# Two mixtures of experts: transposes moved a product ahead, a fixed VectorE order at the end, two tiles of returned rows added by a diagonal product, and next weights that wait for the rows

## The chip, the cores and the metric

The kernel runs on one core of one Trainium2 chip. The metric is device time in microseconds, the median of several runs. TensorE does the matrix products and the transposes, VectorE, ScalarE and GpSimd the rest, and SyncE issues the plain weight loads. In the profile these engines are PE (with PEld for its weight loads), DVE, ACT, POOL and SP.

## The reference, cut to what matters

A network of four layers works on x, 512 rows of 768 float32 values. Each layer adds a graph network and an attention-like mixer, both of the layer-normalised x, and then a feed-forward part, again of the layer-normalised x. The feed-forward parts of layers 0 and 2 are mixtures of experts; these two are what the change touches. With `xt` the normalised rows (512 x 768), 8 experts and a hidden width of 384:

```python
logits = xt @ Ws + bs
routes = argmax(softmax(logits), axis=-1)            # one expert for each row
prob_max = max(softmax(logits), axis=-1)
h = act(xt @ W1[routes] + b1[routes])                # gelu in layer 0, silu in layer 2
out = (h @ W2[routes] + b2[routes]) * prob_max
x = x + out
```

The next layer begins with a layer norm of this x.

## The kernel before, in words

x stays in SBUF as four tiles of 128 rows. A mixture (`moe`, L681) first writes the normalised x to DRAM (`there`), computes each row's expert, and sorts the rows by expert into blocks of 128 places, so that a block belongs to one expert. There are at least 4 and at most 11 blocks; blocks 0 to 8 are always computed (NA is 9), blocks 9 and 10 only under an `If` that reads their number from a register (L862, L869). Each engine reads that register and branches for itself.

Block i has two halves. `first(i)` (L826) gathers the block's rows `xb` and its expert's two weight matrices `w1` and `w2` by indirect DMAs on POOL's queue, transposes `xb` in six pieces into `xbT`, multiplies by `w1` (12 passes, since a float32 product takes two) and copies the result to `h`. `second(i)` (L844) transposes `h` in three pieces, applies the activation and bias on ScalarE (`hT`, L850), multiplies by `w2` (12 passes) and copies the result to `y`, half by VectorE and half by ScalarE (`copy`, L230). ScalarE's queue then stores `y` in DRAM (`back`, L859). The weights go into six buffers of the pool `wp`, shared with all other weight loads.

The loop at L864 calls `first(i + 1)`, then `second_bias` (a product with the 8-row bias table that is added to x, L815), then `second(i)`. So TensorE's order for one turn is: transposes of `xb(i+1)`, `w1(i+1)`, bias, transposes of `h(i)`, `w2(i)`. Instructions run in that order on the engine; a product that reads a copy has to wait for the engine that makes it.

After the loop come the `If`, four gathers of finished rows (`yb`, one for each tile of x, L875) from `back`, and `second(8)`. Block 8 isn't stored: its rows go straight to their places by a product with a placement matrix, `wayT` (L881), 16 passes in all. For every tile VectorE adds the two halves of that product to x (L360) and then the gathered rows times a factor `left`, which is zero for rows of block 8 (L883). What sets VectorE's order here is a scheduler with planned times, which mixes these additions with the statistics of the next norm.

The next norm (`norm1`, L344: two `bn_stats`, `bn_aggr`, a square root on ScalarE, a reciprocal, and on VectorE the scaled copy `xn`) belongs to the next stage. After layer 0's mixture that stage starts with `fold` (L1070 ff.): 72 passes of six weight tiles `g_t` with a small padded matrix `wq`, which POOL fills with a memset (L1075) and a copy (L1076). Its passes use tiles 1 to 3 in the first half and 4 to 6 in the second. Then `xn` is transposed. After layer 2's mixture the stage (`last_two`, L1398) begins with the norm, a small product of `wf` and `lr` (`fold3`, L1466), twelve small VectorE copies `V` out of it (L1482), and the transposes of `xn`. In both cases SyncE's queue issues six weight tiles ahead (L242), each as soon as one of the six `wp` buffers is free.

Of the kernel before, what the change touches and what calls it, by code (L numbers as in the profile page):

```python
# [10 lines left out]
F32 = mybir.dt.float32  # L11
BF16 = mybir.dt.bfloat16
I16 = mybir.dt.int16
I32 = mybir.dt.int32
AF = mybir.ActivationFunctionType
OP = mybir.AluOpType
# [4 lines left out]
P = 128  # L21
N = 512
NT = N // P
# [141 lines left out]
class Net:  # L165
    def __init__(self, ctx, tc, dram, at, out):
# [41 lines left out]
        self.onesb = keep.tile([P, P], BF16, name="onesb")  # L208
        nc.gpsimd.memset(self.onesb, 1.0)
        self.lower = keep.tile([P, P], BF16, name="lower")  # L210
        with tc.tile_pool(name="init", bufs=1) as ip:
# [26 lines left out]
    def w(self, ap, pool=None):  # L238

        parts, n = ap.shape  # L240
        t = (pool or self.wp).tile([P, WB], F32, tag="w", name="w")
        self.nc.sync.dma_start(t[:parts, :n], ap)  # L242
        return t
# [119 lines left out]
    def counts(self, c0, g0):  # L363
# [10 lines left out]
        with ExitStack() as c:  # L374
# [13 lines left out]
            worth = one.tile([P, 3, EJ], F32, name="worth")  # L388
            add = one.tile([P, EJ], F32, name="add")
            for n, ((e, u), (f, v)) in enumerate((((3, 0), (3, 1)), ((3, 2), (3, 3)), ((2, 0), (2, 1)))):  # L390
# [58 lines left out]
            for h in range(2):  # L449
                digit = {}  # L450
                for g in range(2):
# [29 lines left out]
                    for q in range((2 * h + g) * EJ // 8, (2 * h + g + 1) * EJ // 8):  # L481
                        features(q)
        over = self.small.tile([P, NT], BF16, name="over")
        nc.vector.tensor_scalar(over, most, 256.0, None, OP.is_gt)
# [144 lines left out]
    def attention0(self, nodesT):  # L629
        nc, tc, d = self.nc, self.tc, self.d  # L630
        ns = self.chunks(nodesT)
        with ExitStack() as c:
            att = c.enter_context(tc.tile_pool(name="g0_att", bufs=1))
            two = c.enter_context(tc.tile_pool(name="g0_two", bufs=2))
            masks = self.masks(c.enter_context(tc.tile_pool(name="mk", bufs=2)))
            v = att.tile([P, NT, D], F32, name="v")
# [43 lines left out]

    def moe(self, f, act, bs=None):  # L681

# [4 lines left out]
        with ExitStack() as c:  # L687
            one = c.enter_context(tc.tile_pool(name=f + "_one", bufs=1))
            two = c.enter_context(tc.tile_pool(name=f + "_two", bufs=2))
            xn = one.tile([P, NT, D], F32, name="xn")  # L690
            xnT = one.tile([P, KC, N], F32, name="xnT")
# [119 lines left out]
            nc.vector.tensor_copy(wayT, p)  # L811
            nc.vector.tensor_mul(left, left, pr)
            b2 = self.row(d[f + "_b2"], parts=8)

# [10 lines left out]

            def first(i):  # L826
                xb = two.tile([P, D], F32, name="xb", bufs=3)
                nc.gpsimd.indirect_dma_start(out=xb, out_offset=None, in_=there,
                                             in_offset=bass.IndirectOffsetOnAxis(ap=who[:, i : i + 1], axis=0))
                w1 = pick(d[f + "_w1"], i).rearrange("p (k n) -> p k n", k=KC)  # L830
                w2 = pick(d[f + "_w2"], i).rearrange("p (k n) -> p k n", k=3)
                xbT = two.tile([P, KC, P], F32, name="xbT")
                for k in range(0, KC, 3):
                    p = self.ps()
                    for j in range(3):
                        self.tr(p[:, j * P : (j + 1) * P], xb[:, (k + j) * P : (k + j + 1) * P])
                    self.copy(xbT[:, k : k + 3, :], p[:, :HW].rearrange("p (k n) -> p k n", k=3))
                p = self.ps()
                self.acc(p[:, :HW], [(xbT[:, k, :], w1[:, k, :]) for k in range(KC)])
                h = two.tile([P, HW], F32, name="h" if i < NA else "hm")  # L840
                self.copy(h, p[:, :HW])
                return h, w2

            def second(i, h, w2):  # L844
                hT = two.tile([P, 3, P], F32, name="hT")
                p = self.ps()
                for k in range(3):
                    self.tr(p[:, k * P : (k + 1) * P], h[:, k * P : (k + 1) * P])
                for k in range(3):
                    nc.scalar.activation(hT[:, k, :], p[:, k * P : (k + 1) * P], act, bias=bias[:, i, k, :])  # L850
                y = two.tile([P, D], F32, name="y")
                for nb in range(2):
# [8 lines left out]

            count = nc.values_load(more[:1], min_val=4, max_val=NB)  # L862
            held = first(0)
            for i in range(NA - 1):  # L864
                after = first(i + 1)
                second_bias(i // 2, i % 2)
                second(i, *held)
                held = after
            with tc.If(count > NA):  # L869
                for i in range(NA, NB):  # L870
                    second(i, *first(i))
            ys = []
            for t in range(NT):
                ys.append(two.tile([P, D], F32, name="yb", bufs=NT))
                nc.gpsimd.indirect_dma_start(out=ys[t], out_offset=None, in_=back,  # L875
                                             in_offset=bass.IndirectOffsetOnAxis(ap=slot[:, t : t + 1], axis=0))
            y = second(NA - 1, *held)
            for t in range(NT):
                for nb in range(2):
                    p = self.ps()  # L880
                    self.acc(p[:, :HW], [(wayT[:, t * P : (t + 1) * P], y[:, nb * HW : (nb + 1) * HW])])  # L881
                    self.add_x(t, nb, p[:, :HW])
                nc.vector.scalar_tensor_tensor(self.x[:, t, :], ys[t], left[:, t, :], self.x[:, t, :], OP.mult, OP.add)  # L883

# [184 lines left out]

    def fold(self, pool, l, H):  # L1070


        nc, d = self.nc, self.d
        wq = pool.tile([P, KC, 32], F32, name="wq")
        nc.gpsimd.memset(wq, 0.0)  # L1075
        nc.gpsimd.tensor_copy(wq[:, :, : 2 * H], self.col(f"g1_qk{l}", 0, KC * 2 * H).rearrange("p (k h) -> p k h", k=KC))  # L1076

# [119 lines left out]
    def gnn1(self, V1, xnT):  # L1197
        nc, tc, d = self.nc, self.tc, self.d
        with ExitStack() as c:
# [30 lines left out]

            products, turn2 = self.fold(one, 2, 1)
            with tc.tile_pool(name="g1_ex", bufs=2) as self.elu:
# [165 lines left out]
    def last_two(self, xn, xnT, out):  # L1398
# [5 lines left out]
        with ExitStack() as c:  # L1404
            one = c.enter_context(tc.tile_pool(name="m3_one", bufs=1))
            two = c.enter_context(tc.tile_pool(name="m3_two", bufs=2))
            self.norm(self.x, xn)
            V = self.fold3(one)
# [388 lines left out]
def tile_net(ctx, tc, dram, at, out, only=ALL):  # L1797
# [10 lines left out]
    with ExitStack() as ck, ExitStack() as c0:  # L1808
# [15 lines left out]
        if "gnn0" in only:  # L1824
            net.attention0(nodesT)
    if "ffn0" in only:
        net.moe("f0", AF.Gelu, "f0_bs")
    with tc.tile_pool(name="L1", bufs=1) as pool, ExitStack() as keep:
        xnT = pool.tile([P, KC, N], F32, name="xnT")
        right = keep.enter_context(tc.tile_pool(name="L1n", bufs=1, side="right"))  # L1830
        xn = right.tile([P, NT, D], F32, name="xn")
        aT = right.tile([P, KC, N], F32, name="aT")
        V1 = pool.tile([P, KC, 3, 8], F32, name="V1")
        products, turn = net.fold(right, 1, 4)
        net.norm(net.x, xn)
        vt = products(right)
# [9 lines left out]
    with tc.tile_pool(name="L2", bufs=1) as pool:  # L1846
# [3 lines left out]
        if "gnn2" in only:  # L1850
            net.gnn2(xn, xnT)
    if "ffn2" in only:
        net.moe("f2", AF.Silu)
    with tc.tile_pool(name="f3_x", bufs=1) as last:

        xn = last.tile([P, NT, D], F32, name="xn")
        xnT = last.tile([P, KC, N], F32, name="xnT")
        net.ffn3(xn, xnT, net.last_two(xn, xnT, xn))
# [23 lines left out]
```

## Time and profile before

| | |
|---|---|
| median of 3 runs | 4313.59 us (4308.73 to 4316.22) |
| the profiled execution | 4315.56 us, span 4313.8 us, mean granted TensorE clock 0.986 |
| layer 0's mixture, first `xb` transposes to the end of `w2(7)` | 1253.8 to 1351.05 us of the span |
| its end: `fold` starts, `fold` ends | 1373.80, 1383.53 us |
| layer 2's mixture, the same | 2845.0 to 2939.76 us |
| its end: last `xn` done, first product of the next stage with `xnT` | 2967.06, 2969.66 us |
| last stage: first weight load issued | 3168.83 us |

In a timeline, a line is a group of like instructions of one engine: start and length in microseconds, engine, line of the kernel, operation, output and inputs, number of instructions, and in brackets the engine's idle time before it and what ended it. The ends of matmuls are modelled: a row's end lies a little after the moment when the next product could start. The granted clock is 1.00 at full speed and 0.50[...].

### The profile page before, as it was taken

What the parts mean: (1) busy time and instruction counts of PE and PEld (TensorE: products, weight loads), DVE (VectorE), ACT (ScalarE), POOL (GpSimd) and SP (SyncE); (2) the same over time, 40 slices, a digit from 0 to 9 for tenths busy, and PEclk for the clock granted to TensorE, in tenths of its full rate; (3) what the DMA queues carried; (4) which work ended last, traced back from release to release, by engine and by line L of the source; (5) the groups of instructions that cost most, each with busy time, mean ns of one, the idle gap of its engine ahead of it and who ended that gap; (6) DMA issues with size and microseconds to landing.
All of it is one profiled execution on the core that took longest, in us unless ns stands there. A gap on an engine that the chain in (4) does not pass through costs nothing. (4 is left out here: it accounts for less than half of the span.)

```text
span 4313.8 us, 40131 instructions
## 1 busy us (share of the span) xinstructions
PE 4125.5 (96%) x16376; PEld 2099.9 (49%) x16376; DVE 1305.0 (30%) x3120; ACT 650.1 (15%) x1233; POOL 270.3 (6%) x316
## 2 busy tenths in 40 slices
PE   7989999999988999999999999978989999999998
PEld 3434555554444666755644444444554444444443
DVE  7772111112332125623220101035752122122211
ACT  2121200001211223421200000012610000000000
POOL 1120000001022010000000000021100000000000
PEclk9999999999989999999999999989999999999999
DMA  3111011111047112211211111063069999999998
GB/s 110 52 62 56 22 44 66 66 55 53 20 178 269 44 63 71 99 52 46 105 43 66 44 56 55 0 255 129 12 257 419 419 420 420 420 417 420 419 421 362
DMA packets 98956, 710.30 MB, mean 165 GB/s; under 512 B 12032, under 2 KB 12097, under 8 KB 29393
## 3 DMA queue, kind: packets, MB, share of 16 engines
q1 hardware_dynamic: 77776, 601.13, 35.1%
q0 software_dynamic: 16512, 93.97, 5.8%
q10 hardware_dynamic: 4480, 12.58, 0.8%
q8 instruction: 132, 2.16, 0.2%
q14 instruction: 56, 0.45, 0.0%
HBM read 685.09 MB, written 22.54 MB: 164 GB/s over the span
## 5 line engine op out<-in xcount | busy, mean ns | idle before, releaser
L1724 PE MATMUL ps<-w,xg 128*64 128x384 f32 x3072 | 566.0, 489 | 4.2 <-DMA w<-in_f_Wg_dram 2.1
L1724 PEld LDWEIGHTS ps<-w,xg 128*64 128x64 f32 x3072 | 234.1, 137 | 296.2 <-issue 271.1
L1356 PE MATMUL ps<-aT,w 128*128 128x512 f32 x864 | 372.3, 592 | 0.0
L1740 PE MATMUL ps<-w,hT 128*64 128x384 f32 x1536 | 320.7, 490 | 7.4 <-DMA w<-in_f_Wd_dram 3.1
L312 PE MATMUL ps<-xnT,w 128*128 128x512 f32 (+1 forms) x732 | 322.6, 598 | 0.2 <-ACT xnT L236 0.2
L1356 PEld LDWEIGHTS ps<-aT,w 128*128 128x128 f32 x864 | 164.2, 190 | 203.6 <-issue 202.3
L360 DVE TENSOR_TENSOR x<-x,ps 128x384 f32<-128x384 f32 x240 | 131.6, 552 | 329.6 <-PE ps L312 259.6
L312 PE MATMUL ps<-w,xnT 128*128 128x384 f32 x672 | 221.7, 486 | 0.2 <-DVE xnT L234 0.2
L312 PEld LDWEIGHTS ps<-xnT,w 128*128 128x128 f32 (+1 forms) x732 | 134.5, 185 | 175.9 <-issue 172.4
L1740 PEld LDWEIGHTS ps<-w,hT 128*64 128x64 f32 x1536 | 131.9, 136 | 170.8 <-issue 145.0
L312 PE MATMUL ps<-w,hT 128*128 128x384 f32 x552 | 189.4, 499 | 8.8 <-ACT hT L850 8.8
L312 PE MATMUL ps<-C,parts 128*128 128x512 bf16 x864 | 188.8, 380 | 2.5 <-DVE inv L1378 2.5
L463 PE MATMUL ps<-ohd,so 128*128 128x512 bf16 x816 | 182.1, 383 | 2.8 <-DVE so L460 2.8
L312 PEld LDWEIGHTS ps<-w,xnT 128*128 128x128 f32 x672 | 127.0, 190 | 88.6 <-issue 4.8
L1366 DVE TENSOR_TENSOR aT<-inv,ps 128x512 f32<-128x512 f32 x72 | 49.4, 686 | 365.7 <-PE ps L312 365.7
L1727 ACT ACTIVATE h<-ps 128x384 f32<-128x384 f32 x64 | 31.4, 490 | 794.0 <-PE ps L1724 794.0
L1728 DVE TENSOR_TENSOR h<-h,ps 128x384 f32<-128x384 f32 x64 | 35.4, 553 | 376.5 <-PE ps L1724 369.3
L312 PEld LDWEIGHTS ps<-w,hT 128*128 128x128 f32 x552 | 105.4, 194 | 83.9 <-ACT hT L850 13.7
L312 PE MATMUL ps<-w,aT 128*128 128x384 f32 (+1 forms) x416 | 139.6, 486 | 0.5 <-DVE aT L234 0.4
L312 PEld LDWEIGHTS <-parts 128*128 128x128 bf16 x864 | 84.8, 98 | 108.1 <-issue 8.8
L312 PE MATMUL ps<-xnT,sw 128*128 128x512 f32 x288 | 136.7, 605 | 0.0
L460 DVE TENSOR_SCALAR so<-io,ind,worth 128x256 bf16<-128x256 int16 x408 | 121.7, 356 | 35.6 <-PE ps L463 35.5
(487 smaller groups left out, 4787.7 us busy)
## 6 DMA issues: line engine op xcount, KB each, us to landing
w<-in_f_Wg_dram SPq DMA_DIRECT2D x128, 1152.0 KB, 14.5
w<-in_f_Wu_dram SPq DMA_DIRECT2D x128, 1152.0 KB, 14.4
w<-in_f_Wd_dram SPq DMA_DIRECT2D x128, 1152.0 KB, 15.2
w<-in_g_w_dram SPq DMA_DIRECT2D x54, 1152.0 KB, 5.1
w<-in_m_wqkv_dram SPq DMA_DIRECT2D x24, 1152.0 KB, 6.7
w<-in_g_t_dram SPq DMA_DIRECT2D x12, 1152.0 KB, 5.6
w<-in_m_wp_dram SPq DMA_DIRECT2D x8, 1152.0 KB, 5.3
ea<-in_edge_attr_dram SPq DMA_DIRECT2D x34, 256.0 KB, 2.7
```

What stands on the lines that cost most here:

```text
L312: self.nc.tensor.matmul(out, a, b, start=n == 0, stop=n == len(pairs) - 1)
L360: self.nc.vector.tensor_add(xs, xs, p)
L460: nc.vector.tensor_scalar(so[:, n, :], io[:, h * 256 : (h + 1) * 256], ind[:, 0, j : j + 1], worth[:, n, j : j + 1], OP.is_equal, OP.mult)
L463: nc.tensor.matmul(p, so[:, n, t * P : (t + 1) * P], ohd[:, j, :], start=False, stop=j == (g + 1) * HJ - 1)
L1356: nc.tensor.matmul(outs[nb * 3 + f], w[:, k, f * P : (f + 1) * P], xT[:, k, :], start=first and k == 0, stop=last and k == KC - 1)
L1366: nc.vector.tensor_mul(aT[:, f, :], inv[:, r, :], p)
L1724: nc.tensor.matmul(p[a * 64 : a * 64 + 64, :HW], xg[:, k, a * CAP : (a + 1) * CAP], ws[b][a][:, k, :], start=k == 0, stop=k == KC - 1)
L1727: nc.scalar.activation(h, pg[:, :HW], AF.Silu)
L1728: nc.vector.tensor_mul(h, h, pu[:, :HW])
L1740: nc.tensor.matmul(po[nb][a * 64 : a * 64 + 64, :HW], hT[:, f * P + a * 64 : f * P + a * 64 + 64], wd[a][:, f, nb * HW : (nb + 1) * HW], s ...
```

## The change

- The expert loop. `first` is split into `fetch` (gathers and the transposes of `xb`) and the product with `w1`; `second` is split into `middle` (the transposes of `h` and the activation) and the product with `w2`. One turn is now: `middle(i)`, `w1(i+1)`, `fetch(i+2)`, bias, `w2(i)`. `middle(8)` stands ahead of the `If`. The blocks under the `If` have their own `hTm` buffer.
- The end. The eight halves of the placement product go into eight PSUM tiles, all issued one after another. For tiles 2 and 3 of x, the gathered rows are added in the same PSUM tiles by a product with a diagonal matrix that holds `left` (`diag`); tiles 0 and 1 keep VectorE's multiply-add. VectorE's order is written out: each of its instructions is told to be issued after the one before it (`turn`). The next norm is part of this sequence, and its scaled copy moves to ScalarE as an Identity activation with scale r and bias -mean r.
- Next weights. The fifth of the plain weight loads that follow the mixture gets a dependence on the last gather of returned rows; the sixth and later ones stand behind it on SyncE's queue.
- The padded matrix of layer 1's `fold`, now `wq1`, is filled near the start of the program and kept.
- `xn` is a tile of the caller, on the other side of SBUF in layer 0. A small tile `add` in the first stage shares the rotating buffers called `so`, and `over` moves to a lasting pool.

```diff
 def w(self, ap, pool=None):
-    self.nc.sync.dma_start(t[:parts, :n], ap)
+    i = self.nc.sync.dma_start(t[:parts, :n], ap)
+    if self.gate is not None:
+        if self.before == 0:
+            self.tc.add_manual_dep(i.ins, self.gate.name, mybir.DependencyInfo(
+                mybir.DependencyClass.Sync, mybir.DependencyReason.DATA), reason="rows first")
+            self.gate = None
+        self.before -= 1
...
+            diag = one.tile([P, 2, P], F32, name="diag")
+            for t in range(2):
+                nc.vector.tensor_scalar(diag[:, t, :], self.ident, left[:, 2 + t, :], None, OP.mult)
...
-            held = first(0)
+            xbT, w1, w2 = fetch(0)
+            h = first(0, xbT, w1)
+            ahead = fetch(1)
             for i in range(NA - 1):
-                after = first(i + 1)
+                hT = middle(i, h)
+                xbT, w1, after = ahead
+                h = first(i + 1, xbT, w1)
+                if i + 2 < NA:
+                    ahead = fetch(i + 2)
                 second_bias(i // 2, i % 2)
-                second(i, *held)
-                held = after
+                second(i, hT, w2)
+                w2 = after
+            hT = middle(NA - 1, h)
...
-            y = second(NA - 1, *held)
+            self.gate, self.before = i.ins, 4
+            y = second(NA - 1, hT, w2)
+            halves = [(t, slice(nb * HW, (nb + 1) * HW)) for t in range(NT) for nb in range(2)]
+            ps = [self.ps()[:, :HW] for _ in halves]
+            for p, (t, at) in zip(ps, halves):
+                nc.tensor.matmul(p, wayT[:, t * P : (t + 1) * P], y[:, at], start=True, stop=t < 2)
+            for p, (t, at) in zip(ps, halves):
+                if t >= 2:
+                    nc.tensor.matmul(p, diag[:, t - 2, :], ys[t][:, at], start=False, stop=True)
...
+            def end():
+                t, mv, r = held
+                turn(V.reciprocal, r, r)
+                turn(V.scalar_tensor_tensor, mv[:, 0:1], mv[:, 0:1], -1.0, r, OP.mult, OP.mult)
+                nc.scalar.activation(xn[:, t, :], self.x[:, t, :], AF.Identity, bias=mv[:, 0:1], scale=r)
             for t in range(NT):
+                x = self.x[:, t, :]
                 for nb in range(2):
-                    p = self.ps()
-                    self.acc(p[:, :HW], [(wayT[:, t * P : (t + 1) * P], y[:, nb * HW : (nb + 1) * HW])])
-                    self.add_x(t, nb, p[:, :HW])
-                nc.vector.scalar_tensor_tensor(self.x[:, t, :], ys[t], left[:, t, :], self.x[:, t, :], OP.mult, OP.add)
+                    at = slice(nb * HW, (nb + 1) * HW)
+                    turn(V.tensor_add, x[:, at], x[:, at], ps[2 * t + nb])
+                if held:
+                    end()
+                if t < 2:
+                    turn(V.scalar_tensor_tensor, x, ys[t], left[:, t, :], x, OP.mult, OP.add)
...
+                for h in range(2):
+                    turn(V.bn_stats, st[:, h, :], x[:, h * HW : (h + 1) * HW])
+                turn(V.bn_aggr, mv, st)
+                nc.scalar.activation(r, mv[:, 1:2], AF.Sqrt, bias=self.eps)
+                held = t, mv, r
+            end()
```

## The prediction

> **What bounds the kernel now.** I read the page first, then the timeline of the two mixtures and of what follows them, then the waits and the granted clock in short windows there.
>
> ```profile
> span 4313.8 us, 40131 instructions
> PE 4125.5 (96%) x16376; PEld 2099.9 (49%) x16376; DVE 1305.0 (30%) x3120; ACT 650.1 (15%) x1233; POOL 270.3 (6%) x316
> DMA  3111011111047112211211111063069999999998
> ```
>
> TensorE is busy 96% of the span. Only the last quarter is bound by DMA (nines in the DMA line), and that stage begins when the stage before it ends: its first weight load is issued at 3168.83 us, with the DMAs nearly idle from 3040 to 3140. So a microsecond that TensorE's path loses or gains in a mixture should reach the end whole.
>
> One turn of layer 0's expert loop, TensorE's rows of the timeline:
>
> ```profile
> 1284.81 0.82 PE L317 MATMUL ps<-ident,xb 128*128 128x128 f32 x6
> 1285.87 4.14 PE L312 MATMUL ps<-w,xbT 128*128 128x384 f32 x12 [0.24 <-ACT xbT L236]
> 1289.94 0.91 PE L312 MATMUL ps<-row,gT 8*128 8x384 f32 x2
> 1290.78 0.55 PE L317 MATMUL ps<-ident,h 128*128 128x128 f32 x3
> 1291.78 4.14 PE L312 MATMUL ps<-w,hT 128*128 128x384 f32 x12 [0.46 <-ACT hT L850]
> ```
>
> The brackets are the point: twice a turn TensorE transposes something and then stands until its copy is made. Turns last 10.94 and 11.08 us in alternation. No bracket names a weight load: in this window the DMA share is 0.83 at 287 GB/s, against 420 in the last stage.
>
> The ends of the two mixtures, timeline, all engines:
>
> ```profile
> 1354.21 7.18 PE L312 MATMUL ps<-w,hT 128*128 128x384 f32 x12 [0.52 <-ACT hT L850]
> 1358.80 1.00 POOL L875 DMA_INDIRECT yb<-f_back,slot  x1 [11.98 <-DMA f_back<-y]
> 1369.64 1.02 DVE L883 SCALAR_TENSOR_TENSOR x<-yb,left,x 128x768 f32<-128x768 f32 x1 [1.09 <-DMA yb<-f_back,slot]
> 1373.80 9.73 PE L1086 MATMUL ps<-w,wq 128*32 128x384 f32 x72 [6.92 <-POOL wq L1076]
> ...
> 2942.55 4.14 PE L312 MATMUL ps<-w,hT 128*128 128x384 f32 x12 [0.52 <-ACT hT L850]
> 2953.20 1.02 DVE L883 SCALAR_TENSOR_TENSOR x<-yb,left,x 128x768 f32<-128x768 f32 x1 [4.39 <-DMA yb<-f_back,slot]
> 2964.52 0.59 PE L312 MATMUL ps<-lr,wf 64*128 64x24 f32 x2 [12.44 <-DVE xn L355]
> 2966.38 0.68 DVE L355 TENSOR_SCALAR xn<-x,mv,rs 128x768 f32<-128x768 f32 x1
> ```
>
> TensorE stands idle for 6.9 and 12.4 us: in layer 0 until POOL has filled `wq`, in layer 2 until VectorE has added all rows and normalised them.
>
> [...] the granted clock falls at 1353.5, recovers at 1360.3, falls at 1370.6 and recovers at 1377.4, all multiples of 3.41 us apart. That is why the product at 1354.21 took 7.18 us and its like at 2942.55 took 4.14[...]. [...] the store of `y(7)`, issued at 1351.79 just behind a weight load at 1351.08, landed after about 7 us, while the quickest such store took 2.4.
>
> **The change, part by part.** The sum is made against the profiled span of 4313.8 us.
>
> *Loop.* Seen one by one, the starts of the products of this turn are 0.32 us apart within a product and 0.11 within transposes, but 0.51 from the last `xb` transpose to `w1` and 0.73 from the last `h` transpose to `w2`, and in both cases the second pass follows 0.43 after the first. Excess: 0.40 + 0.11 + 0.62 + 0.11 = 1.24 us; 1.37 in the other, longer kind of turn. In the new order the copy of `xbT` has the bias and `w2` ahead of its use (5 us), and the activation has `w1`, transposes and bias (6 us), against 0.5 and 0.9 us that they take. Both waits go. The products stay the same. New seams cost something: around the 8-row bias product starts are 0.42 apart, 0.10 over the pitch, so I take 0.1 off 1.3. Gain 1.2 a turn (0.9 to 1.35), 8 turns, 2 mixtures: 19.2 us (14.4 to 21.6). The weight buffers are freed in the same order, so their loads keep a lead of about two turns (issued 1274.17, used 1296.95).
>
> *Layer 0's first turn.* ScalarE's table load (1.28 us) made `w2(0)` wait 0.93 us, and it then ran at half clock from 1268.2 to 1271.6. That turn took 13.1 us instead of 11. The table load now runs under `w1(1)`: 2.1 us gained (0.9 if the clock drops anyway, 2.6).
>
> *Layer 0's start.* `xn` no longer lies where attention is still reading, so tiles 0 to 2 are normalised during the attention; before, the first waited until 1222.86. The fourth then depends only on its own chain: last addition at 1223.0, statistics and scale 2.65 us, done at 1225.65, against 1228.2. Gain 2.5 us (1 to 2.7).
>
> *The branch.* Zero is the end of `w2(7)` (1351.05; 2939.76). `middle(8)` now stands ahead of the branch, and its three activations delay ScalarE's arrival there by about 0.9 us. TensorE waited for ScalarE there, so it resumes at about +3.1 instead of +2.1 and +1.7, but with `w2(8)` at once; that began at +3.2 and +2.8. Gain 0. If the pause halves the clock, `w2(8)` takes 3 us more; likely in one mixture of two, as before, but before it was hidden behind the gathers.
>
> *The end, layer 0.* The store of `y(7)` goes out at +1.3 instead of +0.7, behind two activations, but no weight load competes: [...]. Gathers are issued 1.25 us apart from +4.4; the quickest took 4.1, so the last lands at +12.3 (before: +18 to +20). TensorE: `w2(8)` to +7.2, placement 5.6 us to +12.8, diagonal 8 passes of 0.32 to +15.4. `fold` no longer waits for POOL: first half (36 passes, 3.85 us at full clock) to +19.2. The second half needs weights 5 and 6, issued from +12.5 and landing [...] at about +20, with POOL's other loads +21.5; so `fold` ends at +24 to +25.4 instead of +32.5. The new norm ends at about +22 and is covered. Gain 7.1 to 8.5; with half clock in one case of two 6.5 (3 to 9).
>
> *The end, layer 2.* VectorE from the first placement half at +7.9: 8 additions of 0.50, 2 multiply-adds of 1.02, 8 `bn_stats` of 0.52, 4 aggregates of 0.24, 8 tiny ones of 0.2, then square root and ScalarE's copy, for 768 columns some 0.85 by its 384- and 512-column rows: 14.1 us. The twelve `V` copies now stand in that order too, and the `wf` load behind them waits until the diagonal products have released its space (+15.4); its product came 3.5 us after its issue, so VectorE stalls about 1 us. Last `xn` at +23, its transposes to +24.2, next product at +24.5 instead of +29.9; at half clock +27. Gain 4 (1 to 6.5). The late weights 5 and 6 are needed tens of microseconds later here: nothing.
>
> *Nothing:* the two `diag` scalings (about 0.25 us each like `way`, while TensorE waits for `xb`), the early `wq1`, `add` in `so`.
>
> Sum: 19.2 + 2.1 + 2.5 + 6.5 + 4 = 34.3 us; low ends 20.3, high ends 42.4. Span 4279.5. The median lies 0.2 us under that profile's span, so 4279 us.
>
> **Rivals.** (a) The loop gives a third: seams or a copy stuck behind ScalarE's store, which waits for VectorE's half of `y`, cost 0.8 a turn. Against it: 4 us of cover. 19.2 - 6.4 = 12.8 less, 4292. (b) The ends give nothing: the store or gathers stay as late as now. At +20 for the last gather, weight 6 comes at +28 and `fold` ends at +32, where it ended before. Against it: the competing loads are gone. 4290. (c) Both: 4302. (d) The scheduler's fixed order or new places in SBUF bring new waits elsewhere, and the net is within 0.2%. The built order outside the mixtures is unchanged. (e) Slower: the new turn puts 0.7 us of transposes beside 0.84 us of an 8-row product. [...] The 157 us of loop would be 52 us longer with every second window at half clock: 4331. From about four fifths of that, 43 us, the change is measurably slower. Against it: the old turn's lull with idle time in it never halved the clock after the first turn.
>
> **Numbers.** Main case 0.60, (a) 0.17, (b) 0.11, (c) 0.04, (d) 0.04, (e) 0.04. A measurement of this kernel can tell about 0.2%, 8.6 us, from no change: the first four are faster, 0.92, (d) the same, 0.04, (e) slower, 0.04. The main case alone spans 4271 to 4293; with (a) and (b), 4268 to 4298.
>
> **What would show it.** Turns of about 9.8 us with no bracket of `xbT` or `hT` ahead of products; layer 0's logits product 2.5 us closer to the end of attention; the first gather within 5 us of the end of `w2(7)`; `fold` starting at about +15 with a pause in its middle for weight 6; the next product of layer 2 at +25. Wrong would be: turns above 10.6 us, a halved clock within the loop, a first gather at +7 or later, or a gain in the mixtures that the stages after them give back.

## The result and the profile after

The changed kernel takes 4281.88 us, median of 4 runs (4280.96 to 4283.03), against 4311.41 us (4308.73 to 4316.22) before: a ratio of 0.9931 with an interval of 0.9919 to 0.9943. The forecast was 4279.0 us in a range of 4268 to 4298. The profiled execution took 4283.03 us with a span of 4281.2 us; that of before had a span of 4313.8 us. So the two traces differ by 32.6 us, some 3 us more than the medians, which differ by 29.5.

The page of the kernel after, its first lines and the DMA line:

```profile
span 4281.2 us, 40171 instructions
...
PE 4117.0 (96%) x16392; PEld 2100.7 (49%) x16392; DVE 1299.7 (30%) x3120; ACT 659.5 (15%) x1241; POOL 268.9 (6%) x316
...
DMA  3111011111047112211201111063079999999998
```

The picture is the same: TensorE busy for 96% and a last quarter that DMA bounds. That quarter begins at 3135.97 us instead of 3168.83 (its first weight load), so nothing gained before it was lost on the way.

One turn of layer 0's loop, timeline of the kernel after, TensorE only:

```profile
1274.08 0.82 PE L325 MATMUL ps<-ident,xb 128*128 128x128 f32 x6
1274.83 0.91 PE L320 MATMUL ps<-row,gT 8*128 8x384 f32 x2
1275.67 4.14 PE L320 MATMUL ps<-w,hT 128*128 128x384 f32 x12
1279.64 0.49 PE L325 MATMUL ps<-ident,h 128*128 128x128 f32 x3
1279.97 4.04 PE L320 MATMUL ps<-w,xbT 128*128 128x384 f32 x12
1283.84 0.82 PE L325 MATMUL ps<-ident,xb 128*128 128x128 f32 x6
```

The same work as before, but no bracket is left: from one group of `xb` transposes to the next are 9.76 us, against 10.94 and 11.08.

The ends, timeline of the kernel after, all engines (zero, as in the prediction, is the end of `w2(7)`, now at 1337.72 in layer 0 and at 2911.86 in layer 2). Layer 0:

```profile
1340.23 4.14 PE L320 MATMUL ps<-w,hT 128*128 128x384 f32 x12 [2.19 <-ACTq L895]
...
1342.56 1.00 POOL L902 DMA_INDIRECT yb<-f_back,slot  x1 [8.07 <-DMA f_back<-y]
...
1350.76 0.82 SPq L244 DMA_DIRECT2D w<-in_g_t_dram  x2
1352.36 4.70 PE L1157 MATMUL ps<-w,wq 128*32 128x384 f32 x38
...
1357.90 1.03 ACT L932 ACTIVATE xn<-x,mv,rs 128x768 f32<-128x768 f32 x1 [0.43 <-DVE mv L923]
...
1361.88 6.56 PE L1157 MATMUL ps<-w,wq 128*32 128x384 f32 x32 [3.76 <-DMA w<-in_g_t_dram]
```

The first gather comes at +4.84 instead of +7.75, and `fold` starts at +14.64 instead of +22.75. But then it stands 3.76 us for weight 6 (SyncE had issued weights 5 and 6 from +13.04 on) and runs its second half in 6.56 us, since the granted clock was 0.50, half speed, from 1360.13 to 1366.96 us. It ends at +30.7, where it ended at +32.5 before. Layer 2:

```profile
2926.65 0.56 POOL L1541 DMA_DIRECT2D wf<-in_g_wf_dram  x1 [6.29 <-DVE x L923]
...
2932.79 0.59 PE L320 MATMUL ps<-lr,wf 64*128 64x24 f32 x2 [6.79 <-DMA lr<-in_g_lr_dram]
2933.48 0.15 DVE L1552 COPY V<-ps 64x2 f32<-64x2 f32 x1 [4.33 <-PE ps L320]
2933.73 1.03 ACT L932 ACTIVATE xn<-x,mv,rs 128x768 f32<-128x768 f32 x1 [5.21 <-DVE mv L923]
...
2938.30 5.31 PE L320 MATMUL ps<-xnT,V 128*24 128x512 f32 x12 [0.33 <-DVE xnT L236]
```

VectorE stands 4.33 us ahead of the first `V` copy, and the last two `xn` wait behind it: that copy needs the product of `wf` and `lr`, and `lr`, issued only at +15.3, is used 5.6 us later. The next product starts at +26.44 instead of +29.90.

Where the 32.6 us of the two traces went, by the same points in both (first `xb` transposes, end of `w2(7)`, first product with `xnT` of the next stage, first load of the last stage):

| stretch | before, us | after, us | gained |
|---|---|---|---|
| to layer 0's first `xb` transposes | 1253.80 | 1251.35 | 2.45 |
| layer 0, from there to the end of `w2(7)` | 97.25 | 86.37 | 10.88 |
| layer 0, from there to the next stage's first product | 35.58 | 33.83 | 1.75 |
| layers 1 and 2 up to layer 2's logits product | 1433.98 | 1430.21 | 3.77 |
| from there to the first `xb` transposes | 24.39 | 24.26 | 0.13 |
| layer 2, from there to the end of `w2(7)` | 94.76 | 85.84 | 8.92 |
| layer 2, from there to the next stage's first product | 29.90 | 26.44 | 3.46 |
| from there to the last stage's first weight load | 199.17 | 197.67 | 1.50 |
| the last stage | 1144.97 | 1145.23 | -0.26 |

The mixtures gave 27.6 us. Another 5.0 us come from stretches that the change doesn't touch; the last section comes back to the larger part of them.

### The profile page after: what moved, and what is told of

It is laid out like the page before. It is cut to its first block, busy times and chain, and to the rows that moved or that the text cites. A ratio compares the mean times of both kernels' runs of the same rounds, so it can differ in the third digit from the quotient of the medians.

```text
span 4281.2 us, 40171 instructions
## 1 busy us (share of the span) xinstructions
PE 4117.0 (96%) x16392; PEld 2100.7 (49%) x16392; DVE 1299.7 (30%) x3120; ACT 659.5 (15%) x1241; POOL 268.9 (6%) x316
```

## The experiments

My theory after this comparison: the loop is two thirds of the gain and stands on its own; the ends gave little, because the late weights stop `fold` in layer 0, and because VectorE stands behind the `V` copies in layer 2. The rivals are in the expectations. Below, "fold ends" and "product, layer 0" (the first product of the next stage with `xnT`, which comes behind `fold`) are counted from the end of `w2(7)` in layer 0, "product, layer 2" (the next product, as above) from its end in layer 2. The last column is the stretch of layers 1 and 2 from the table above, whose TensorE instructions are the same in all of them. All columns but the medians come from one profiled execution of each kernel.

| kernel | median, us (lowest to highest) | fold ends | product, layer 0 | product, layer 2 | layers 1 and 2 |
|---|---|---|---|---|---|
| before | 4311.41 (4308.73 to 4316.22) | +32.48 | +35.58 | +29.90 | 1433.98 |
| the change | 4281.88 (4280.96 to 4283.03) | +30.72 | +33.83 | +26.44 | 1430.21 |
| loop alone | 4289.12 (4288.08 to 4290.77) | +32.79 | +35.89 | +31.87 | 1430.14 |
| loop undone | 4299.05 (4297.68 to 4303.10) | +25.82 | +30.63 | +26.38 | 1433.55 |
| no wait of the weights | 4286.26 (4281.82 to 4287.54) | +28.83 | +34.30 | +30.54 | 1431.89 |
| wait for the first tile | 4280.67 (4278.71 to 4281.89) | +25.74 | +31.40 | +29.19 | 1430.99 |
| V copies early | 4276.53 (4273.15 to 4277.62) | +30.07 | +33.17 | +22.38 | 1429.25 |
| V early, second tile in layer 0 | 4273.46 (4272.05 to 4276.85) | +24.99 | +29.81 | +22.06 | 1429.26 |
| no diagonal products | 4282.25 (4279.71 to 4283.67) | +24.79 | +28.19 | +28.81 | 1433.90 |
| no fixed order | 4279.12 (4277.83 to 4280.68) | +28.91 | +32.02 | +27.89 | 1430.52 |
| small loads later | 4278.93 (4277.69 to 4280.36) | +25.20 | +28.30 | +28.19 | 1433.67 |
| V early, second tile, small loads later | 4273.34 (4272.20 to 4276.48) | +24.36 | +27.46 | +22.03 | 1433.38 |

The change was timed beside runs of before with a median of 4311.41 us, the ten kernels below it beside runs of before with 4309.36 to 4309.97 us. So a total that differs from the change's by some 2 us shows nothing by itself, and larger differences are given below against the runs of before as well.

**The loop alone, and everything but the loop.** To the kernel before, only `fetch`, `first`, `middle`, `second` and the new loop were added; the other way round, the changed kernel got the old ones back:

```diff
-            held = first(0)
+            xbT, w1, w2 = fetch(0)
+            h = first(0, xbT, w1)
+            ahead = fetch(1)
...
-            y = second(NA - 1, *held)
+            y = second(NA - 1, hT, w2)
```

> The kernel before with the new order of the expert loop alone; starts and ends of the mixtures as before. Theory (the loop's two waits are the gain, and they do not depend on the ends): turns of 9.76 us without a bracket, about 10.9 us gained between the first xb transposes and the end of w2(7) in layer 0 and about 9 in layer 2, so 4311.4 - 20 = about 4291 us (4287 to 4296, since a pause can meet another clock window later). Rival (the loop's gain is kept only because the ends no longer wait for gathers and POOL, which take it back otherwise): turns of 9.76 us, but the ends grow by as much, above 4300 us.

> The changed kernel with the old order of the loop; everything else of the change stays. Theory: turns of 10.94 and 11.08 us with brackets for xbT and hT, and 4281.9 + 20 = about 4302 us (4297 to 4306). Rival (start and ends carry next to nothing): 4308 to 4312 us. The start of layer 0 keeps its 2.5 us in both.

The loop alone takes 4289.12 us, a ratio to before of 0.9950 (0.9934 to 0.9967), 21 us less than the runs of before beside it. With the loop undone the time is 4299.05 us, a ratio to before of 0.9975 (0.9964 to 0.9987), and 17 us more than the change (19 when each is set against its own runs of before). (In layers 1 and 2, which the loop doesn't touch, the profiled executions of these pairs differ by 3.8 and 3.3 us.) Turns are 9.76 us in the first. In the second the brackets are back, in the timeline of TensorE:

```profile
1285.41 4.14 PE L320 MATMUL ps<-w,hT 128*128 128x384 f32 x12 [0.46 <-ACT hT L862]
...
1290.58 4.14 PE L320 MATMUL ps<-w,xbT 128*128 128x384 f32 x12 [0.38 <-DVE xbT L236]
```

So the loop's gain does not need the new ends. The rival has a small share: with the loop alone, layer 2's next product comes at +31.87 instead of +29.90, since gathers start at +10.84 instead of +7.81 (and at +9.46 in layer 0). The loop undone also shows the start: from the start of attention's last addition to layer 0's logits product are 5.92 us before and with the loop alone, and 3.81 with the loop undone. So 2.1 us are gained here without the new loop. They fit the place of `xn`: in the change the first three `xn` tiles are transposed in one row ahead of the fourth. But no run moved `xn` alone.

**The wait of the weights.** Left out altogether, or moved to the first gathered tile:

```diff
-            self.gate, self.before = i.ins, 4
```

```diff
+                i0 = i if t == 0 else i0
...
-            self.gate, self.before = i.ins, 4
+            self.gate, self.before = i0.ins, 4
```

> The changed kernel without the wait of the next weights for the last gathered rows. Theory (the wait costs more in layer 0 than it gains): weights 5 and 6 are issued at the ends of w2(7) and w2(8), at about +0 and +7 instead of +13.0; the store of y(7) and the gathers get later by 2 to 4 us, the diagonal products start at about +15 instead of +12.0, but fold then runs through without its pause of 4 us and ends at +23 to +27 instead of +30.7. In layer 2 lr comes back in under 4 us instead of 5.5, with the next product at +25 to +28 instead of +26.4. Total 4274 to 4281 us. Rival (the rows are what the end waits for, and weights ahead of them hold them back as in the kernel before): first gather at +7 or later, diagonal products at +19, fold ends at +30 or later, total 4282 us or more.

> The changed kernel, with the next weights waiting for the first gathered tile of rows instead of the last. Theory: weights 5 and 6 are issued at about +8.5 instead of +13.0, after the store of y(7) has landed; weight 6 is there at about +17, so fold's pause of 4 us shrinks to under 0.5 and fold ends at +23 to +26 instead of +30.7, while the gathers behind the first lose at most 1.5 us. In layer 2 the loads of wf and lr meet less traffic, and VectorE's stall of 4.3 us before the V copies shrinks to about 2. Total 4272 to 4278 us. Rival (it is the traffic beside the gathers that counts, whichever time the weights start): diagonal products later by 4 us, total 4282 us or more.

Both totals missed my theory: without the wait the kernel is slower by 4.4 us in the medians (the ranges just overlap; 5.8 when each is set against its own runs of before), with the earlier one it is 1.2 us faster, which is within the spread. The two mixtures go opposite ways. Without the wait, layer 2, timeline of TensorE and POOL (zero at 2911.54):

```profile
2920.08 0.95 POOL L902 DMA_INDIRECT yb<-f_back,slot  x1 [31.76 <-issue]
...
2927.75 5.49 PE L912 MATMUL ps<-yb,diag 128*128 128x384 f32 x8 [4.89 <-DMA yb<-f_back,slot]
...
2942.08 3.16 PE L320 MATMUL ps<-xnT,V 128*24 128x512 f32 x7 [0.33 <-DVE xnT L236]
```

The first gather slips from +3.78 to +8.54, the diagonal products from +11.40 to +16.21, the next product from +26.44 to +30.54. There the rival is right: the store of `y(7)` and the gathers behind it lose 4 to 5 us to the weights that are moved beside them. In layer 0 the gather slips too (+7.71 instead of +4.84), and `fold` starts only at +20.80, yet it ends 1.9 us sooner than in the change, since it then runs through. The next stage gains nothing from that. Its first product has to wait for its own first weight, which is loaded behind `fold`'s, and comes at +34.30 instead of +33.83. Layer 0, timeline of TensorE (zero at 1335.32):

```profile
1369.62 10.64 PE L320 MATMUL ps<-w,xnT 128*128 128x384 f32 x27 [2.20 <-DMA w<-in_m_wqkv_dram]
```

With the wait on the first tile, `fold` in layer 0 starts at +17.80 and ends 5 us sooner than in the change, and the next stage starts 2.4 us sooner, again after a wait of 2.39 us for its own weight; in layer 2 the last gathered tile's diagonal product waits until +17.59, where all were under way from +11.40 in the change, and the next product is 2.8 us later. So one wait serves two places with different needs: in layer 2 nobody asks for the weights soon, in layer 0 `fold` does, and behind it the next stage.

**No diagonal products.** VectorE adds all four tiles' rows with its multiply-add; the two `diag` scalings and eight passes go:

```diff
-                nc.tensor.matmul(p, wayT[:, t * P : (t + 1) * P], y[:, at], start=True, stop=t < 2)
+                nc.tensor.matmul(p, wayT[:, t * P : (t + 1) * P], y[:, at], start=True, stop=True)
...
-                if t < 2:
+                if t < NT:
                     turn(V.scalar_tensor_tensor, x, ys[t], left[:, t, :], x, OP.mult, OP.add)
```

> The changed kernel without the diagonal products: VectorE adds all four tiles of rows with multiply-adds of 1.02 us, as in the kernel before, in the fixed order. Theory (the diagonal product takes 2 us from VectorE and gives TensorE a wait for the rows): in layer 0 fold starts at about +12.5 instead of +14.6 but still ends at about +30.7, since weights 5 and 6 are as late as now; in layer 2 the next product starts 1 to 2.5 us later than +26.4. Total 4282 to 4285 us. Rival (the diagonal products bring nothing, since VectorE stands for 4.3 us at the V copies anyway): layer 2's next product at +26.4 or sooner, 4280 to 4282 us. A third, that they are needed for the gain of the end: more than 4 us slower.

In layer 2 the next product comes at +28.81 instead of +26.44, as expected, and the total is the same within the spread. (The 2.4 us are no more than a hint: the same end of layer 2 as in the change gave +26.38 in one of the other runs and +28.19 in another.) But `fold` in layer 0 did not end at +30.7. Timeline of POOL, SyncE and TensorE, zero at 1336.63:

```profile
1348.76 0.82 SPq L244 DMA_DIRECT2D w<-in_g_t_dram  x2
...
1356.96 0.53 POOL L1060 MEMSET rf<- 128x512 f32 x1 [11.53 <-ACT xn L929]
...
1357.36 4.06 PE L1154 MATMUL ps<-w,wq 128*32 128x384 f32 x32 [1.96 <-DMA w<-in_g_t_dram]
...
1363.86 0.82 PE L325 MATMUL ps<-ident,xn 128*128 128x128 f32 x6
```

The weights were issued at +12.13, 0.9 us sooner than in the change, but weight 6 was there 8.6 us after that, and not 11.1. What had moved is POOL: its memset of `rf`, and the small loads of layer 1 behind it, stood until +20.3 instead of +14.9. This gave the next experiment. (Here the last `xn` becomes the limit, its six transposes starting at +27.2; the next stage still begins 5.6 us sooner than in the change. Layers 1 and 2 then took 3.7 us more.)

**Layer 1's small loads behind weight 6.** `ga`, `rf`, `be` and the two masks, 0.06 to 0.5 MB each, get a dependence on the sixth weight load:

```diff
+    def behind(self, i):
+        if self.sixth:
+            self.tc.add_manual_dep(i.ins, self.sixth, mybir.DependencyInfo(
+                mybir.DependencyClass.Sync, mybir.DependencyReason.DATA), reason="weights first")
...
-            nc.gpsimd.memset(rf, -0.5)
+            self.sixth = self.latest.ins.name
+            self.behind(nc.gpsimd.memset(rf, -0.5))
```

> The changed kernel, with layer 1's small loads on POOL (ga, rf, be and the first two masks) waiting until weight 6 has landed; the weights still wait for the last gathered tile. Theory (weight 6 is late for two reasons of about equal size: it is issued only at +13.0, and beside it the small loads are moved): weight 6 is there at +19 to +20.5 instead of +24.2, so fold's second half starts then and at full clock, and fold ends at +23 to +25 instead of +30.7; layer 2 is as in the changed kernel (next product at about +26.4). Total 4275 to 4279 us. Rival (the two weights need their 11 us by themselves, whatever is beside them): weight 6 at +23 or later, fold ends at +28 or later, total as the changed kernel within 2 us.

Timeline, zero at 1336.02:

```profile
1348.43 0.82 SPq L244 DMA_DIRECT2D w<-in_g_t_dram  x2
...
1357.16 4.06 PE L1165 MATMUL ps<-w,wq 128*32 128x384 f32 x32 [1.78 <-DMA w<-in_g_t_dram]
1357.17 0.53 POOL L1071 MEMSET rf<- 128x512 f32 x1 [6.03 <-DMA w<-in_g_t_dram]
```

Weight 6 comes 8.7 us after its issue (+21.1; I had said +19 to +20.5), `fold` stands for 1.8 us instead of 3.8, keeps its full clock (4.06 us for the same 32 passes instead of 6.56), and ends at +25.2, 5.5 us sooner. So of the 11.1 us from issue to use in the change, up to 2.4 are the small loads. The share is not a fixed one: in the other kernels with these loads where `fold` had to wait, the time was 10.1 to 10.9 us. In the two versions at the end of this section, where two gathers still move beside the weights, it is 10.3 us with them and 9.9 without. The rest is the two weights and what else moves beside them.

The clock differs with the pause. In the traces of before and of the change all changes of the granted clock lie whole multiples of 3.41 us apart (those of the change at 1237.25, 1257.73, 1360.13 and 1366.96 us, for example, 6, 30 and 2 of them), and so mark windows out. Those around the pause (length, busy time of PE, PEld, DVE, ACT and POOL, granted clock, DMA share, GB/s), first in the change, then with the small loads later:

```profile
1356.72:1360.13 3.41, 1.18 (x4) 0.14 (x2) 0.71 (x4) 1.64 (x3) 0.00 (x0) 1.00 1.01 340
1360.13:1363.55 3.42, 1.67 (x9) 0.57 (x12) 0.00 (x0) 0.00 (x0) 0.00 (x0) 0.50 0.98 364
...
1354.75:1358.16 3.41, 1.63 (x14) 0.40 (x13) 0.81 (x4) 1.73 (x3) 0.99 (x2) 1.00 0.91 316
1358.16:1361.58 3.42, 3.42 (x30) 1.39 (x25) 0.00 (x0) 0.80 (x2) 2.79 (x6) 1.00 1.01 423
```

In the change the clock fell to 0.50 behind a window in which TensorE was busy for 1.18 us. With the shorter pause TensorE was busy for 1.63 us in the window, and the clock stayed at 1.00.

**The fixed order.** The dependence of each VectorE instruction on the one before it is left out:

```diff
-                if last is None:
+                if True:
                     last = fn(*args).ins
```

> The changed kernel without the fixed order of VectorE's instructions at the end of the mixtures: the scheduler places the two multiply-adds third and eighth, ahead of statistics that need no gathered rows, and all twelve V copies behind the additions as now. Theory (the order is worth little: in both versions VectorE ends behind the same V copies, and in layer 0 fold waits for weights): layer 0's fold ends at about +30.7, layer 2's next product at +26 to +28 instead of +26.4; total 4281 to 4284 us. Rival (the fixed order is what lets the norms start before all rows are in): layer 2's next product at +29 or later, total 4285 us or more.

The next product of layer 2 comes at +27.89 instead of +26.44 and `fold` ends at +28.91; in the total there is no loss (4279.12 us). A worth of the order can't be read from this: 1.5 us in layer 2 are within what the same code differs by, and the scheduler's order has the same stall before the `V` copies, 4.47 us. The rival, which wanted +29 or later, falls.

**The V copies early.** Layer 2's `fold3` became a generator, called in turns 2 (loads) and 5 (product, copies) of the expert loop, with its tiles in the caller's pool:

```diff
+                if also and i in (2, 5):
+                    next(also)
                 second(i, hT, w2)
...
-            V = self.fold3(one)
```

> The changed kernel, with layer 2's small loads wf and lr, their product and the twelve V copies made in the middle of that mixture's expert loop, in space of their own. Theory (in the changed kernel VectorE's fixed order stands for 4.3 us behind the V copies, whose loads meet the late weights): the stall at the V copies is gone, the last xn of layer 2 is done at about +21 instead of +25.0 and the next product starts at +22.5 to +23.5 instead of +26.4 after the end of w2(7); layer 0's end does not change (fold ends at about +30.7). Total 4281.9 - 3.5 = about 4278 us (4276 to 4281), if no pause later meets another clock window. Rival (the stall only covers VectorE's or the gathers' own time): next product at +25.5 or later, 4281 to 4283 us.

Layer 2's end, timeline of ScalarE and TensorE, zero at 2909.15:

```profile
2928.98 1.03 ACT L934 ACTIVATE xn<-x,mv,rs 128x768 f32<-128x768 f32 x1 [0.42 <-DVE mv L925]
...
2930.06 1.54 PE L325 MATMUL ps<-ident,xn 128*128 128x128 f32 x6 [0.35 <-ACT xn L934]
...
2931.53 1.05 PE L320 MATMUL ps<-xnT,V 128*24 128x512 f32 x1
```

The last `xn` is done at +20.9 and the next product starts at +22.38, 4.1 us sooner than in the change. The total, 4276.53 us, is 5.4 us less than that of the change, or 3.6 when each is set against its own runs of before. The stall covered nothing else.

**Both causes mended.** The same with the weights in layer 0 behind the second gathered tile (in layer 2 behind the last, as in the change), and then also with the small loads later:

```diff
+                gate = i if t <= (1 if f == "f0" else NT - 1) else gate
...
-            self.gate, self.before = i.ins, 4
+            self.gate, self.before = gate.ins, 4
```

> The changed kernel with the V copies early, as above, and in layer 0 the next weights waiting for the second gathered tile instead of the last; in layer 2 they wait for the last as in the change. Theory (in layer 0 the weights are what fold waits for, in layer 2 nothing waits for them): in layer 0 the weights are issued at about +10 instead of +13, tile 3's gather loses about 1.5 us, fold starts at about +16 and ends at +23 to +25 instead of +30.7; in layer 2 the next product starts at +22.5 to +23.5. Total 4281.9 - 6.5 - 3.5 = about 4272 us (4269 to 4276). Rival (what is gained at the end of a mixture is lost again in later pauses and clock windows): 4278 to 4283 us.

> All of what helped so far: V copies early, layer 0's weights behind the second gathered tile, layer 1's small loads behind weight 6. Theory: in layer 0 weight 6 is there at +17.5 to +19, fold starts at about +14.7 and runs through to +22.5 to +23.5; in layer 2 the next product starts at about +22.2. Against the version with the first two of these (4273.5 us, fold to +25.0) 2 us less: 4269 to 4274 us. Rival (at this size the gain is drowned by which clock window the later pauses meet, which moved identical work by up to 4.7 us between the runs): 4272 to 4277 us.

The first takes 4273.46 us, a ratio to before of 0.9916 (0.9900 to 0.9933), and beats the changed kernel by 8.4 us, or 6.7 when each is set against its own runs of before; its runs, 4272.05 to 4276.85, lie below all runs of the change. In its timeline (zero at 1336.09) the weights are issued at +10.63 and the second half of `fold` stands for 1.56 us:

```profile
1350.76 4.71 PE L1160 MATMUL ps<-w,wq 128*32 128x384 f32 x40
...
1357.03 4.06 PE L1160 MATMUL ps<-w,wq 128*32 128x384 f32 x32 [1.56 <-DMA w<-in_g_t_dram]
```

With the small loads later as well, `fold` has no pause left:

```profile
1352.07 8.00 PE L1168 MATMUL ps<-w,wq 128*32 128x384 f32 x72
```

But it starts 1.7 us later, because `w2(8)` took 5.83 us instead of 4.14 (as long as `w2(0)` took before, with the granted clock at 0.50 for 3.41 us of it), and ends at +24.36 instead of +24.99. Weight 6 was there at +20.4, later than the +17.5 to +19 that I had expected. The next stage starts at +27.46 instead of +29.81, since it no longer waits 1.55 us for its own weight: the 2.4 us are there at their place. Yet the total is the same, 4273.34 us, which is the rival of that expectation: layers 1 and 2 took 4.1 us more in the profiled execution of this version than of the other.

## Why the prediction was right, point by point

The time was right, and so was the mechanism that carries it. But the sum of 34.3 us was made for the mixtures alone, which gave 27.6 in the traces; 5.0 us came from elsewhere. The close hit is partly luck.

- *Loop, 19.2 us, and first turn, 2.1 us:* right. Turns are 9.76 us; both mixtures' loops with their first turns gave 10.9 + 8.9 = 19.8 us in the traces. The working of the turn held in each term. What is missing is in the first `w1(0)`, which caught more of a halved clock: 6.52 us instead of 5.43 in layer 0 and 5.97 instead of 5.15 in layer 2 (4.04 later in the loop). Taken alone or taken away, the loop is worth 21 and 17 us.
- *Layer 0's start, 2.5 us:* right; 2.45 us to the first `xb` transposes, of which 2.1 lie between the last addition and the logits product.
- *The branch, 0:* TensorE waited until +2.51 and +2.03, not +3.1, and gained 0.65 and 0.76 us. The activations of `middle(8)` delayed ScalarE's arrival by 0.3 to 0.4 us, not by 0.9, and the store of `y(7)` goes out at +0.73 and +0.54, not at +1.3.
- *The end of layer 0, 6.5 us (3 to 9):* this step failed. It gave 1.75 us. The gathers (first at +4.84; I said +4.4, by my estimate of the store's landing), the placement and the diagonal products came as worked out, and `fold` started at +14.64 for a forecast of +15.4. The failing term is the landing of weight 6. I took +20, and +21.5 with POOL's other loads; its passes started at +24.16, 11.1 us after the issue. From that follow both a pause of 3.76 us and two clock windows at half speed, 2.5 us more. Against the forecast of +25.4 for `fold`'s end, 2.7 us are the later landing and 2.5 the clock. The 7.5 us from issue to landing in my +20, and the 9 in my +21.5, were my estimate; no trace showed them. With the small loads later, the two weights took 8.7 us; with them, 11.1. With the loop undone, `fold` starts at +17.04 and ran without a pause, and the end of layer 0 gave 5.0 us (+30.63 instead of +35.58).
- *The end of layer 2, 4 us:* the size is right at 3.46 us, one term in it isn't. VectorE stood for 4.33 us at the `V` copies where I had said 1. I took `lr`'s time from the kernel before, where the weights had not been held back until just ahead of it. The runs show two parts: where `lr` was used 2.2 to 2.3 us after its issue (no wait, first tile, no diagonal products), VectorE still stood 2.2 to 3.4 us, because the load is issued only shortly before VectorE arrives; where `lr` took 4.9 to 5.9 us, the stall was 3.6 to 5.5. With that stall gone the next product came at +22.4 and +22.1. "The late weights are needed tens of microseconds later here: nothing" is right for the weights and wrong for `lr`, which is loaded beside them and was used 5.6 us after its issue. The next product at +26.4 lies between my +24.5 and +27, but only since I had left room for a halved clock; what came late was the last `xn`, at +25.0 for a forecast of +23.
- *Nothing elsewhere:* the rest of the program was not expected to move, and moved by 5.0 us, below.
- *The clock:* the spacing of its changes is as I read it, 3.41 us and multiples, in the trace of the change too. In the window ahead of the fall at 1353.5, 1350.15 to 1353.56, TensorE was busy for 1.31 us.
- *Rivals:* (a), and with it (c), falls with the turns of 9.76 us; (d) falls with the interval, which ends at 0.9943; (b), the ends give nothing, is half true for layer 0, though by another way than late gathers; (e) falls, no turn at half clock after the first ones (the granted clock of the change was 1.00 from 1257.73 to 1360.13 us and from 2831.28 to 2930.26).

## What to carry to other kernels

A wait that clears the way for one transfer moves another one later: ask what is next in line for the delayed one, and what is being loaded by then. The same wait gained 4.1 us in one mixture; in the other it made `fold` end 1.9 us later, and the next stage began only 0.5 us sooner than without it. If a consumer stands close behind, release the load at the earliest point that still leaves the urgent transfer its way, and measure at the stage behind the consumer, not at the consumer alone. And before writing out an engine's order, look for small instructions in it that depend on a load which has not been issued yet.

## What was unexpected: the same work in other clock windows

Layers 1 and 2 up to the logits run the same TensorE instructions in all twelve kernels, yet took 1429.3 to 1434.0 us in the profiled execution of each (the last column of the table). Here are the same 36 passes, before and after (the columns as above):

```profile
1453.90:1463.80 9.90, 9.54 (x36) 7.36 (x36) 0.76 (x3) 2.31 (x5) 0.00 (x0) 0.66 0.00 0
```

```profile
1438.81:1445.37 6.56, 6.20 (x36) 4.92 (x36) 0.76 (x3) 2.32 (x5) 0.00 (x0) 1.00 0.00 0
```

The granted clock differs over the whole stretch. Before, it was 0.50 for 19.8 us of it, 6.83 of them at this place (1455.96 to 1462.79); in the change for 10.2 us, and not here. Its mean over the stretch reads 0.99 in the five kernels with 1433.4 us and more (before, loop undone, no diagonal products, small loads later, and the last one) and in the one that waits for the first tile (1430.99 us), and 1.00 in the other six. At this place it was 0.69 without diagonal products (1434.8 to 1444.8 us) and 1.00 with V early and the second tile (1435.9 to 1445.9). Between before and the change the stretch makes 3.8 of the 5.0 us from elsewhere.

In both traces there is a pause of 0.52 us shortly before. What differs is how it lies in the windows of 3.41 us: before, it ends at 1453.23, early in the window from 1452.55 to 1455.96; after, at 1438.14, late in the one from 1435.23 to 1438.64. The window ahead of the fall and the one behind it, before:

```profile
1452.55:1455.96 3.41, 2.54 (x21) 2.26 (x21) 0.00 (x0) 1.85 (x5) 0.00 (x0) 1.00 0.16 68
1455.96:1459.38 3.42, 3.42 (x15) 3.15 (x15) 0.76 (x3) 0.00 (x0) 0.00 (x0) 0.50 0.00 0
```

Between 1200 and 3150 us the traces of before and after have 19 such windows at full clock with a halving behind them. In 17 of them TensorE was busy for at most 1.34 us. The other two are in the trace of before, this one with 2.54 us and the one that ends at 1268.23 with 2.48. In the kernel after, TensorE was busy for 2.89 and 3.05 us in the windows over the same passes, 1435.23 to 1438.64 and 1438.64 to 1442.05, and the clock stayed at 1.00. Why it fell behind 2.54 us isn't shown.

No run here moved a pause on purpose, and there is one profile of each kernel, so it isn't shown whether another execution of the same kernel would fall the same way. What is measured is the size: 4.7 us between the traces over this stretch, and 197.2 to 200.8 us for the stretch from layer 2's next product to the last stage. A gain of 2 us at one place, like that of the last version, can't be told from the total; it has to be read at its place.
